# Attention's first steps in a four-layer adapter kernel: VectorE's order written out, token sums behind the divisors, a transfer split over two queues

## The chip, the cores and the metric

The kernel runs on one core of one Trainium2 chip. The metric is the device time of one execution in microseconds (us), as a median over runs. A profiled execution gives the trace that is read here; its engines are TensorE (PE; its weight loads are listed as PEld), VectorE (DVE), ScalarE (ACT), GpSimd (POOL) and SyncE (SP), which issues transfers.

## What is computed

Four residual layers over `x` of 8 sequences x 128 tokens x 512 features, all in float32: each is `x = x + ffn(cond(x))`. Layer 0 is a gated feed-forward network with low-rank adapters and a mixture of eight low-rank experts; layer 1 is an adapter and again eight experts; layer 2 is attention with a paged cache of keys and values, followed by a mixture; layer 3 is routed experts. The change lies at the end of layer 1 and in layer 2's attention:

```python
q = rope(rmsnorm(x @ Wq.T, q_norm_w), pos)          # 32 heads of 128
k = rope(rmsnorm(x @ Wk.T, k_norm_w), pos)          # 8 heads of 128
v = x @ Wv.T
kc, vc = k_cache[block_table], v_cache[block_table]  # 512 cached tokens, 8 heads
scores = q @ concat(kc, k).T / sqrt(128)             # cached tokens past the length masked
x = x + mixture(softmax(scores) @ concat(vc, v) @ Wo.T)
```

## The kernel before

**Steps.** Attention goes over 8 key heads (`qd`), and within one over 4 pairs of sequences (`p`): 32 steps `n`, each with two sequences `j` and four query heads. The projections of a step are a 2 x 2 block product done with seven products instead of eight (`seven`, lines 948 to 988): it needs sums of weight blocks (`factors`, line 871) and sums of token blocks (`tokens`, line 930, computed by `combine`, line 923). `seven` has named places (`one`, `u2`, `c22`, `c11`, `c12`) at which a caller can put other work into the program's order. After a projection come `squares` (ScalarE, sums of squares), `rotate` (products with the sine tables on GpSimd, line 1051; with the cosine tables on VectorE, line 1056), `roots` (ScalarE), `rotated` and `normed` (VectorE, lines 1068 to 1080) and `turn` (line 1103): VectorE transposes blocks of 32 x 32 of the queries and new keys into one tile, `written` (line 1096) sends that to DRAM in four transfers and `fetch` (line 1112) reads it back with the head dimension on the partitions. The cached keys go the same way in `turn_cached` (line 1087); both tiles share one buffer, the tag `kt` with `bufs=1`. `gather` (line 907) fetches cached keys and values by rows with GpSimd's transfers.

**A turn of the loop** (`run`, line 1254): `weigh` makes scores for one sequence, five key blocks each, and ScalarE takes their exponentials (lines 1124 and 1128); `added` sums the five blocks on VectorE (line 1144); `mix` multiplies with the values (line 1175); `summed` gets the divisors on TensorE (line 1153); `inverted` takes their reciprocals (line 1160), copies them into `R` (line 1163) and spreads them over the partitions with three transfers (line 1165). In the next step `divided` (line 1185) applies `R`, `outputs` computes the block sums `os` of the result, and `leave` is a second `seven` product with the output weights that adds into `y2`. Step `n`'s turn projects step `n+1`, and prepares the cached keys and token sums of step `n+2`.

**What sets the order.** Each engine runs its instructions in the order in which the build lists them. The build is free to reorder what is ready by its own reckoning, except that instructions passed to `keep_in_program_order` keep their order among themselves on their engine. `kept` (line 853) passes an instruction there if `running` is not empty, if its engine is GpSimd, or if `always` is given. `running` becomes true only in `run`, after steps 0 and 1 have been projected; so the first two steps' projections are ordered by the build, together with layer 1's expert products (`outs1`, TensorE and a sum into `x` on VectorE, line 300), which are never kept. Layer 1's experts end with `mix1(1)` (four transposes on TensorE and a copy) and `outs1(1)` (four products, whose banks have the tag `st` with three buffers; `seven`'s second product uses one of these too).

**First steps in the program's text before.** `att.first(0)` has step 0's token sums, projection, squares, rotation, the keys' gather for step 1, roots, turning and fetching; then `mix1(1)` and `outs1(1)`; then `run` calls `first(1)` for step 1. In the loop, step 0 computes `tokens(2)` and then `turn_cached(1)`, whose read of the cached keys is issued ahead of `fetch(1)`. Steps from 1 on compute `tokens(n + 2)` between `added` and `summed`, hence before `inverted`. There are token sums only where `qd` of step `n+2` is 0, 1 or 7: from 2 to 6 the sums of 1 are kept.

Of the kernel before, what the change touches and what calls it, by code (L numbers as in the profile page):

```python
# [17 lines left out]
P = 128  # L18
# [29 lines left out]
def forward(ctx: ExitStack, tc: tile.TileContext, a: dict, out: bass.AP):  # L48
# [615 lines left out]
    with psa:  # L664
# [46 lines left out]
        route1(1)  # L711
        att.first(0)
        mix1(1, small_bank)
        outs1(1, range(DC), large_bank)
        kept = nc.dram_tensor("kept_x", (P, DC, NT), F32, kind="Internal").ap()
# [70 lines left out]
def attention(tc, a, x, ident, lens, kvrow, part, ww, wop, ypool, sums, rot, eps, psa, c2, chunks, mm):  # L786
# [65 lines left out]

    def kept(i, always=False):
        return tc.keep_in_program_order(i) if always or running or i.ins.engine == pool.engine else i

# [37 lines left out]
    def every(ops):  # L893
        for _ in ops:
            pass
# [33 lines left out]

    def tokens(n):  # L930


        qd, p = steps[n]
        b = 2 * p
        if 0 < qd < NQ - 1 and p in kept_sums:
            S[n]["A"] = kept_sums[p]
            return
        parts = [x[:, 2 * h : 2 * h + 2, (b + j) * P : (b + j + 1) * P] for j in range(2) for h in range(2)]
        if 0 < qd < NQ - 1:
            if not kept_sums:  # L940
                late.append(late[0].tile([P, NP, 4, 2, P], F32, tag="yT", name="xs_all"))
            S[n]["A"], ops = combine(late[1][:, p], *parts)
            kept_sums[p] = S[n]["A"]
        else:
            S[n]["A"], ops = combine(wk.tile([P, 4, 2, P], F32, tag="xs", name=f"xs_{n}", bufs=1), *parts)
        every(ops)

# [133 lines left out]

    def turn_cached(n, always=False):

        s = S[n]
        t = wk.tile([P, 4, 8, 32], F32, tag="kt", name=f"kt_{n}", bufs=1)
        for j in range(2):
            kept(dve.transpose(
                t[:, :, 4 * j : 4 * j + 4, :], s["kc"][j].rearrange("p c (b d) -> p b c d", b=4)
            ), always)
        s["kT"] = wk.tile([P, 4, 8, 32], F32, tag="kT", name=f"kT_{n}")  # L1090
        written(turned[n], t)
        kept(sp.dma_start(s["kT"], turned[n].rearrange("b i a m d -> (b i) a m d")))

    def written(dst, t):
        for q in range(4):
            kept(sp.dma_start(dst[:, :, q].rearrange("b i m d -> i b m d"), t[32 * q : 32 * q + 32]))

    def turn(n):

        s = S[n]  # L1100
        m = 2 * REP
        t = wk.tile([P, 4, m + 2, 32], F32, tag="kt", name=f"qkt_{n}", bufs=1)
        kept(dve.transpose(t, s["both"].rearrange("p m (b d) -> p b m d", b=4)))
        s["qT"] = wk.tile([P, 4, m, 32], F32, tag="qT", name=f"qT_{n}", bufs=1)
        s["kn"] = wk.tile([P, 2, 4, 32], F32, tag="kTn", name=f"kTn_{n}", bufs=1)
        written(turned_new[n], t)

    def fetch(n):
        s = S[n]
        m = 2 * REP  # L1110
        src = turned_new[n].rearrange("b i a m d -> (b i) a m d")
        kept(sp.dma_start(s["qT"], src[:, :, 0:m, :]))
        for j in range(2):
            kept(sp.dma_start(s["kn"][:, j], src[:, :, m + j, :]))
# [122 lines left out]

    def first(n):
        tokens(n)
        project(n, {"u2": lambda: turn_cached(n, True)} if n == 0 else {})  # L1240
        for j in range(2):
            squares(n, "q", j, range(REP))
            squares(n, "k", j, range(1))
        rotate(n)()
        if n == 0:
            gather(1, "k")
        roots(n)
        rotated(n)
        normed(n)
        turn(n)  # L1250
        if n == 0:
            fetch(n)

    def run(pool_, end_of, bank, keep):
# [3 lines left out]
        pool.memset(y2, 0.0)  # L1258
        first(1)
        gather(1, "v")  # L1260
        running.append(True)
        end, prepared = None, iter(())
# [5 lines left out]
        for n, (qd, p) in enumerate(steps):  # L1268
# [3 lines left out]
            sums_of, outs = added(n, 0), iter(())  # L1272
            next(sums_of)
            if n:
                divided(n - 1)
                outs = outputs(n - 1)
                some(w_ops)()
            every(sums_of)
            if after:
                project(after, {  # L1280
                    "one": some(outs, 2),
                    "u2": lambda: (every(outs), every(w_ops), some(wo_ops)()),
                    "c22": lambda: (turn_cached(2) if n == 1 else None, some(wo_ops, 2)()),
                    "c11": lambda: (squares(after, "k", 0, (0,)), squares(after, "q", 0, (0, 1))),
# [19 lines left out]
            else:  # L1304
                tokens(2)
                turn_cached(1)
                gather(2, "k")
# [6 lines left out]
            if n == 0:  # L1314
                fetch(1)
            every(added(n, 1))
            if 0 < n < len(steps) - 2:
                if steps[n + 2][1] == 0:
                    w_ops = W[steps[n + 2][0]].factors()
                    some(w_ops, 2)()  # L1320
                tokens(n + 2)
            summed(n)
# [9 lines left out]
            if 0 < n < len(steps) - 2:  # L1332
                turn_cached(n + 2)
            if n == 3:
# [779 lines left out]
```

## Time and profile before

| | |
|---|---|
| runs before | 1568.65, 1560.52, 1567.32 us; median 1567.32 us |
| profiled execution | 1561.03 us, of which the span is 1559.2 us |
| mean granted TensorE clock | 0.995 |
| instructions | 18584 |
| VectorE, ScalarE, GpSimd busy | 1034.2, 538.1, 827.6 us |
| transfers | 169.89 MB, on average 109 GB/s |

How to read it: a line of the order of time has the start in the span, the duration, the engine, the line of the code, the operation, the tile written and the tiles read, the shapes and a count of like instructions; in brackets stands how long the engine had been idle before it, and what ended that idle time. A product in float32 is two instructions on TensorE. Project, attention and output products of a typical step take some 33 us. Steps 0 and 1 are projected between about 303 and 331 us, step 0's scores begin at 333.9 us, step 1's at 356.0 us, and the last step ends near 1400 us.

### The profile page before, as it was taken

What the parts mean: (1) busy time and instruction counts of PE and PEld (TensorE: products, weight loads), DVE (VectorE), ACT (ScalarE), POOL (GpSimd) and SP (SyncE); (2) the same over time, 40 slices, a digit from 0 to 9 for tenths busy, and PEclk for the clock granted to TensorE, in tenths of its full rate; (3) what the DMA queues carried; (4) which work ended last, traced back from release to release, by engine and by line L of the source; (5) the groups of instructions that cost most, each with busy time, mean ns of one, the idle gap of its engine ahead of it and who ended that gap; (6) DMA issues with size and microseconds to landing.
All of it is one profiled execution on the core that took longest, in us unless ns stands there. A gap on an engine that the chain in (4) does not pass through costs nothing.

```text
span 1559.2 us, 18584 instructions
## 1 busy us (share of the span) xinstructions
PE 1520.0 (97%) x5985; PEld 925.7 (59%) x5985; DVE 1034.2 (66%) x1963; ACT 538.1 (35%) x1324; POOL 827.6 (53%) x842
## 2 busy tenths in 40 slices
PE   9999999989999999999999999999999999999998
PEld 7888886445555555555555555555555555568643
DVE  4566334387787786777777687777777888743241
ACT  1111110143434544444543444543445443420210
POOL 1341105285765777776777766777767677610000
PEclk9999999999999999999999999999999999999999
DMA  9111002144546434553454454355444335421000
GB/s 302 42 42 31 1 0 65 43 118 123 162 118 189 137 108 121 153 174 103 127 159 124 124 145 145 101 149 163 129 137 141 103 101 149 144 65 62 0 21 36
DMA packets 156682, 169.89 MB, mean 109 GB/s; under 512 B 54144, under 2 KB 127040, under 8 KB 156448
## 3 DMA queue, kind: packets, MB, share of 16 engines
q1 hardware_dynamic: 138432, 131.60, 29.9%
q0 software_dynamic: 17056, 36.49, 7.9%
q8 instruction: 50, 0.82, 0.2%
q10 hardware_dynamic: 1088, 0.52, 0.1%
q14 instruction: 56, 0.46, 0.1%
HBM read 113.89 MB, written 42.07 MB: 100 GB/s over the span
## 4 chain that ended last, share of the span: by engine, by line
PE 85%; DVE 5%; DMA 4%; POOL 3%; issue 2%; ACT 1%; SPq 0%; ACTq 0%; DVEq 0%; POOLq 0%
PE st L1124 16%; PE av L1175 15%; PE g L362 8%; PE q_six L962 7%; PE wo_two L962 5%; PE q_one L962 5%; PE dn L362 5%; PE q_five L962 4%; PE wo_six L962 3%; PE wo_one L962 3%; PE eo_l L53 2%; PE z L53 2%; PE h L1679 2%; PE o L53 2%; PE midp_l L53 1%
## 5 line engine op out<-in xcount | busy, mean ns | idle before, releaser
L907 POOL DMA_INDIRECT kn<-in_k_cache,kvrow_k x256 | 282.9, 1105 | 73.3 <-issue 67.1
L1175 PE MATMUL av<-pT,vals 128*128 128x512 f32 x640 | 298.8, 597 | 0.0
L907 POOL DMA_INDIRECT vals<-in_v_cache,kvrow_v x256 | 258.1, 1008 | 73.4 <-issue 44.5
L1128 ACT ACTIVATE pT<-st,hide 128x512 f32<-128x512 f32 x256 | 175.9, 687 | 325.7 <-PE st L1124 325.7
L1124 PE MATMUL st<-qT,kT 128*128 128x512 f32 x512 | 237.7, 597 | 7.2 <-DMA qT<-turned_new 7.2
L1051 POOL TENSOR_TENSOR vq<-q,txq 128x256 f32<-128x256 f32 x128 | 118.7, 956 | 180.8 <-ACT sqq L1035 117.4
L1175 PEld LDWEIGHTS av<-pT,vals 128*128 128x128 f32 x640 | 119.0, 190 | 143.9 <-issue 141.5
L1124 PEld LDWEIGHTS st<-qT,kT 128*128 128x128 f32 x512 | 97.2, 191 | 117.4 <-issue 111.0
L1144 DVE TENSOR_TENSOR part<-pT 128x512 f32<-128x512 f32 x128 | 88.3, 692 | 82.7 <-ACT pT L1128 82.5
L962 PE MATMUL q_one<-q,x 128*128 128x384 f32 x256 | 93.0, 486 | 0.0
L1035 ACT ACTIVATE sqq<-q 128x128 f32<-128x128 f32 x256 | 79.3, 310 | 15.9 <-DVE q L1011 9.1
L1160 DVE RECIPROCAL rr<-sum 128x256 f32<-128x256 f32 x32 | 56.1, 1754 | 31.3 <-PE sum L1153 31.3
L962 PEld LDWEIGHTS q_one<-q,x 128*128 128x128 f32 x256 | 48.5, 190 | 39.8 <-issue 14.3
L962 PE MATMUL q_six<-q_s,xs_all 128*128 128x384 f32 x192 | 69.8, 486 | 0.0
L962 PE MATMUL wo_one<-o,oT 128*128 128x256 f32 x256 | 65.7, 379 | 0.0
L1124 PE MATMUL st<-qT,kTn 128*128 128x512 f32 x128 | 65.4, 592 | 0.0
L1016 ACT COPY q<-q_one 128x256 f32<-128x256 f32 x32 | 11.9, 372 | 153.4 <-PE q_one L962 144.5
L1213 POOL TENSOR_TENSOR y<-y,uo 128x512 f32<-128x512 f32 x32 | 41.3, 1291 | 43.3 <-DVE y L1205 42.8
L962 PE MATMUL wo_two<-o_s,os 128*128 128x256 f32 x256 | 60.5, 379 | 2.3 <-DVE os L923 2.3
L1128 ACT ACTIVATE pT<-st,rs 128x512 f32<-128x512 f32 x64 | 44.0, 687 | 38.4 <-PE st L1124 38.4
L962 PEld LDWEIGHTS wo_one<-o,oT 128*128 128x128 f32 x256 | 48.6, 190 | 13.4 <-PE st L1124 0.4
L1185 DVE TENSOR_TENSOR oT<-av,R 128x512 f32<-128x512 f32 x64 | 41.2, 685 | 21.6 <-DMA R<-R 21.3
(394 smaller groups left out, 2711.4 us busy)
## 6 DMA issues: line engine op xcount, KB each, us to landing
turned_new<-qkt SPq DMA_DIRECT2D x128, 160.0 KB
turned_cached<-kt SPq DMA_DIRECT2D x128, 128.0 KB
kT<-turned_cached SPq DMA_DIRECT2D x32, 512.0 KB
qT<-turned_new SPq DMA_DIRECT2D x32, 512.0 KB
R<-R SPq DMA_DIRECT2D x96, 128.0 KB
q<-in_WqT SPq DMA_DIRECT2D x8, 1024.0 KB
o<-in_WoT SPq DMA_DIRECT2D x8, 1024.0 KB
kn<-in_k_cache,kvrow_k POOLq DMA_INDIRECT x256, 3.0
```

The lines of the kernel that those rows point to most:

```text
L53: pe.matmul(o, lhsT, rhs, start=start, stop=stop)
L362: pe.matmul(o, lhsT, rhs, start=start, stop=stop, skip_group_check=True)
L907: kept(pool.indirect_dma_start(out=d[:, c, :], out_offset=None, in_=kc if what == "k" else vc, in_offset=bass.IndirectOffsetOnAxis(ap=kvro ...
L962: kept(pe.matmul(o, l[:, c, :], r[:, c, :], start=start and c == 0, stop=c == 1, skip_group_check=True))
L1035: kept(act.activation(sq, S[n][m][:, j, i, :], AF.Square, accum_out=S[n]["ssq"][:, j, col : col + 1]))
L1051: kept(pool.tensor_tensor(to, t[:, b, :, hi : hi + 64], wx[:, b, lo : lo + 64].unsqueeze(2).to_broadcast(list(to.shape)), ALU.mult,))
L1124: kept(pe.matmul(ps, s["kT"][:, c, 4 * j : 4 * j + 4, :] if c < 4 else s["kn"][:, j], s["qT"][:, :, REP * j : REP * (j + 1), :].rearrange( ...
L1128: kept(act.activation(pT[:, c, :, :].rearrange("p i t -> p (i t)"), ps, AF.Exp, **(dict(bias=hide[:, b, c : c + 1]) if c < 4 else dict(bia ...
L1144: kept(dve.tensor_tensor(o, l, r, ALU.add))
L1160: kept(dve.reciprocal(r, S[n]["sum"]))
L1175: kept(pe.matmul(ps, v[:, c, :], pT[:, c, :, :].rearrange("p i t -> p (i t)"), start=c == 0, stop=c == NC - 1, skip_group_check=True,))
L1213: kept(pool.tensor_tensor(t, t, u.unsqueeze(1).to_broadcast([P, 2, HW]), ALU.add))
```

## The change

- `first` now covers both first steps. `running` becomes true right after step 0's token sums, so everything in `first` that goes through `kept` holds the program's order.
- Step 1's token sums are computed at `c22` of step 0's projection, into a buffer with the tag `pT` instead of `xs`.
- Step 0's squares lie at `c11` and `c12` of its own projection. After it come `rotate(0)`'s first part, the keys' gather for step 1 and layer 1's `mix1(1)`. Step 1's projection follows, and behind its first product comes the rest of step 0: squares, roots, the keys' products, expert products 0 and 1 between the steps of the rotation, the turning, its four writes from SyncE's and ScalarE's queues in turn, and the fetch. Expert products 2 and 3 follow; their sums into `x` on VectorE are bound to come after the turning.
- `run` begins with three products into a bank that nobody reads (`idle_q`), then step 1's squares, rotation and turning.
- In step 0 of the loop `turn_cached(1)` comes ahead of `tokens(2)`, and the read of its result is issued after the read of step 1's queries instead of before it.
- In the loop, the token sums of step `n+2` move from before `summed` to behind `inverted` and `turn_cached(n + 2)`. A weight sum (`w_ops`) comes before `divided` instead of after it. The first two of the four `os` sums, which were at `one` of the projection, move to `u2` beside the other two.

The diff, without the lines that only follow from these (the argument `always` goes away):

```diff
@@ forward
         route1(1)
-        att.first(0)
-        mix1(1, small_bank)
-        outs1(1, range(DC), large_bank)
+        att.first(lambda: mix1(1, small_bank), lambda *o: outs1(1, o, large_bank))
@@ attention: turn_cached, written, turn, fetch
         written(turned[n], t)
-        kept(sp.dma_start(s["kT"], turned[n].rearrange("b i a m d -> (b i) a m d")))
+        return lambda: kept(sp.dma_start(s["kT"], turned[n].rearrange("b i a m d -> (b i) a m d")))
-    def written(dst, t):
+    def written(dst, t, by=(sp,)):
         for q in range(4):
-            kept(sp.dma_start(dst[:, :, q].rearrange("b i m d -> i b m d"), t[32 * q : 32 * q + 32]))
+            kept(by[q % len(by)].dma_start(dst[:, :, q].rearrange("b i m d -> i b m d"), t[32 * q : 32 * q + 32]))
-    def fetch(n):
+    def fetch(n, between=lambda: None):
         kept(sp.dma_start(s["qT"], src[:, :, 0:m, :]))
+        between()
         for j in range(2):
             kept(sp.dma_start(s["kn"][:, j], src[:, :, m + j, :]))
@@ first
-    def first(n):
-        tokens(n)
-        project(n, {"u2": lambda: turn_cached(n, True)} if n == 0 else {})
-        for j in range(2):
-            squares(n, "q", j, range(REP))
-            squares(n, "k", j, range(1))
-        rotate(n)()
-        if n == 0:
-            gather(1, "k")
-        roots(n)
-        rotated(n)
-        normed(n)
-        turn(n)
-        if n == 0:
-            fetch(n)
+    def first(mixed, outs_):
+        every(tokens(0))
+        running.append(True)
+        later = tokens(1, "pT")
+        project(0, {
+            "u2": lambda: turn_cached(0)(),
+            "c22": lambda: every(later),
+            "c11": lambda: (squares(0, "k", 0, (0,)), squares(0, "q", 0, (0, 1))),
+            "c12": lambda: squares(0, "q", 0, (2, 3)),
+        })
+        keys_terms = rotate(0)
+        gather(1, "k")
+        mixed()
+        def rest():
+            squares(0, "q", 1, range(REP))
+            squares(0, "k", 1, (0,))
+            roots(0)
+            keys_terms()
+            outs_(0)
+            rotated(0)
+            outs_(1)
+            normed(0)
+            turned_0 = turn(0, (sp, act))
+            fetch(0)
+            with tc.issue_after(turned_0.ins):
+                outs_(2, 3)
+        project(1, {"one": rest})
@@ run
-        first(1)
+        idle = psa.tile([P, 512], F32, tag="mm", name="idle_q", bufs=3)
+        for _ in range(3):
+            kept(pe.matmul(idle, x[:, 0, 0:P], x[:, 0, 0:512], start=True, stop=True))
+        for j in range(2):
+            squares(1, "q", j, range(REP))
+            squares(1, "k", j, (0,))
+        rotate(1)()
         gather(1, "v")
-        running.append(True)
+        roots(1)
+        rotated(1)
+        normed(1)
+        turn(1)
...
             next(sums_of)
+            some(w_ops)()
             if n:
                 divided(n - 1)
                 outs = outputs(n - 1)
-                some(w_ops)()
             every(sums_of)
             if after:
                 project(after, {
-                    "one": some(outs, 2),
                     "u2": lambda: (every(outs), every(w_ops), some(wo_ops)()),
...
             else:
-                tokens(2)
-                turn_cached(1)
+                read_cached = turn_cached(1)
+                every(tokens(2))
                 gather(2, "k")
...
             if n == 0:
-                fetch(1)
+                fetch(1, read_cached)
             every(added(n, 1))
-            if 0 < n < len(steps) - 2:
-                if steps[n + 2][1] == 0:
-                    w_ops = W[steps[n + 2][0]].factors()
-                    some(w_ops, 2)()
-                tokens(n + 2)
+            if 0 < n < len(steps) - 2 and steps[n + 2][1] == 0:
+                w_ops = W[steps[n + 2][0]].factors()
+                some(w_ops, 2)()
             summed(n)
             inverted(n)
...
             if 0 < n < len(steps) - 2:
-                turn_cached(n + 2)
+                turn_cached(n + 2)()
+                every(tokens(n + 2))
```

## The prediction

> **What bounds the kernel now.** I read the page's busy times and chain first, then TensorE's waits by releaser, then the order of time around each wait, then the granted clock. TensorE is the bound: the page gives it 97% of the span and 85% of the chain.
>
> ```profile
> PE 1520.0 (97%) x5985; PEld 925.7 (59%) x5985; DVE 1034.2 (66%) x1963; ACT 538.1 (35%) x1324; POOL 827.6 (53%) x842
> ...
> PE 85%; DVE 5%; DMA 4%; POOL 3%; issue 2%; ACT 1%; SPq 0%; ACTq 0%; DVEq 0%; POOLq 0%
> ```
>
> So only TensorE's idle time (1559.2 - 1520.0 = 39.2 us) and time at a lower clock can be won; VectorE's 66% is worth something only where a wait of TensorE ends on it. TensorE's waits (us in total, times, longest):
>
> ```profile
> PE st L1124 <- DMA qT<-turned_new: 7.2, 3, 3.5
> PE q_five L962 <- DVE uq L977: 3.5, 3, 1.2
> PE eo_l L53 <- DVE x L300: 2.4, 1, 2.4
> ...
> PE q_six L962 <- DVE vals L1011: 1.3, 3, 0.5
> ...
> PE q_six L962 <- DVE q_s L871: 0.6, 1, 0.6
> ```
>
> These are the ones that the diff can reach. In order of time, attention's first steps hold three:
>
> ```profile
> 320.48 1.37 PE L53 MATMUL eo_l<-midT_l,wB 128*128 128x512 f32 x2 [2.40 <-DVE x L300]
> ...
> 333.89 5.37 PE L1124 MATMUL st<-qT,kT 128*128 128x512 f32 x8 [3.50 <-DMA qT<-turned_new]
> ...
> 356.02 3.67 PE L1124 MATMUL st<-qT,kT 128*128 128x512 f32 x8 [2.26 <-DMA qT<-turned_new]
> ```
>
> The eight products at 333.89 take 5.37 us, those at 356.02 take 3.67: the clock fell. The busy time by stretch (length, then TensorE, weight load, VectorE, ScalarE, GpSimd, clock) shows two stretches at half clock, one after each of the first two waits:
>
> ```profile
> 321.25:324.60 3.35, 3.35 (x6) 1.70 (x6) 3.35 (x4) 0.00 (x0) 2.74 (x3) 0.50 0.17 54
> ...
> 334.90:338.25 3.35, 3.35 (x6) 1.27 (x5) 3.28 (x6) 1.37 (x2) 2.74 (x3) 0.50 0.17 44
> ```
>
> Each costs some 3.4 x 0.5 = 1.7 us. All that can be won here: 2.40 + 3.50 + 2.26 + 2 x 1.7 = 11.6 us. VectorE in the same time:
>
> ```profile
> 319.74 1.28 DVE L300 TENSOR_TENSOR x<-eo_l,x 128x512 f32<-128x512 f32 x2
> ...
> 323.34 1.50 DVE L1103 STREAM_TRANSPOSE qkt<-r 128x1280 f32<-128x1280 f32 x1
> ...
> 330.97 3.61 DVE L1056 TENSOR_TENSOR r<-q,tsq 128x1024 f32<-128x1024 f32 x1
> ...
> 343.79 1.30 DVE L1087 STREAM_TRANSPOSE kt<-kn 128x512 f32<-128x512 f32 x2
> ```
>
> The first sums into x (line 300) stand behind step 0's whole rotation, so the fourth expert product has no free bank. The turning of step 0's queries ends at 324.84 and TensorE gets them at 333.89, 9.05 us later.
>
> In the loop the other waits lie in three steps in which token sums are computed ahead of the divisors. In one:
>
> ```profile
> 1219.06 1.49 DVE L923 TENSOR_TENSOR xs<-x 128x256 f32<-128x256 f32 x1
> ...
> 1222.01 1.74 DVE L1160 RECIPROCAL rr<-sum 128x256 f32<-128x256 f32 x1
> ...
> 1230.06 1.29 DVE L1185 TENSOR_TENSOR oT<-av,R 128x512 f32<-128x512 f32 x2 [3.00 <-DMA R<-R]
> ```
>
> VectorE sits 3.00 us on R's transfer with all the next projection's sums behind it. TensorE loses 0.65 + 1.20 + 0.51 there, 1.20 + 0.51 at 434.76 and 436.82, 1.06 + 0.24 + 0.21 at 502.88 to 511.63: 5.6 us.
>
> **What the Trainium skill says.** "TensorE: Matmul & The Clock Gate", Part 1: the array falls to half clock after an idle window of about 3.4 us, and the windows run free of the program. The trace agrees in the length (0.50 over 3.35 us and more), but windows only partly idle (2.40 us) were enough here, and the 2.26 us before 356.02 brought no drop. "DMA: Bandwidth & Descriptors", Issuing engines are not separate DMA queues: transfers from several engines share the same DMA engines; only issue time is saved. The trace of before has one queue alone, 1.94 us for four writes. "SBUF — State Buffer", SBUF: two separate sides: VectorE with two inputs in SBUF and GpSimd lock each other out for whole instructions. That fits the 3.61 us product above, beside four GpSimd products; the same form took 1.31 at 370.20.
>
> **The change, part by part.**
>
> *Order in step 0.* Step 1's token sums move ahead of the projection's last sums, two sums into x instead of four stand before the turning, the other two behind. From the trace, the last sum of step 0's projection could end near 313.9 (TensorE ends that projection at 313.1). Then: 1.75 + 0.94 (products with the tables) + 0.69 (x) + 1.47 + 0.43 (rotation) + 0.69 (x) + 0.21 + 1.22 + 1.50 = 8.9, so the turning ends at 322.8, 2.0 earlier. If GpSimd locks it as above (3.61 for 1.75), 324.7, no gain.
>
> *Two queues.* Four issues in 1.94 us become two pairs side by side: at most 1.0 saved, at least 0, as the data share one set of DMA engines. I take 0.5. The two on ScalarE's queue wait for the turning; behind them stand the copies of step 1's queries, which come 8.9 us after ScalarE's last work in before, so that costs nothing; without that cover it would be two issues of 0.49. Scores of step 0 then start at 322.8 + 9.05 - 0.5 = 331.35 instead of 333.89: 2.5 won.
>
> *Expert products and step 1's projection.* The second product of step 1 now waits for the second sum into x, at 313.9 + 1.75 + 0.94 + 0.69 + 1.47 + 0.43 + 0.69 = 319.9; TensorE is through with the expert products at 318.1. An idle of 1.8 stays, but the path to the scores goes through the turning: the projection (6 x 1.29 = 7.7) ends at 327.6, ahead of them. A half clock here costs at most its 1.7 and is covered by that.
>
> *Idle products.* Three of two instructions, 0.43 apart: 2.6 us, 327.6 to 330.2, ahead of the scores in TensorE's queue. They hide under the wait up to 331.35 and leave 1.1 bare. What they buy is the half clock after 333.89: 1.7. Uncovered they would cost 2.6.
>
> *What is late next.* Step 1's rotation now starts near 328.7, not 330.97; its turning took until 339.32, 8.35 later, of which 1.9 is the lock: I take 336.2 (335.2 to 337.1). Its tile has one buffer, which the turning of step 1's cached keys shares and which is free when the four writes have landed, 4.5 later as in step 0 (324.84 to 329.36): 340.7. The change puts those keys ahead of the token sums, so VectorE would stand idle there; then keys 1.3, token sums 1.55, key-block sums 2.78: TensorE can sum the divisors at 346.5. It gets there 13.0 after the scores start (335.6 without the half clock, to 348.63): 344.4. A new wait of 2.1. From there to step 1's scores 5.1 (348.63 to 353.76): 351.6. The query read is now issued ahead of the cached keys' read, which lands by 350 to 352; so the 2.26 goes. 356.02 - 351.6 = 4.4 won in the first steps.
>
> *Token sums behind the divisors; weight sums ahead of the division; output sums after the projection's.* R leaves 3.1 to 4.0 earlier (what the four token sums took in each of those steps), and the token sums fill the wait for it. VectorE's work up to the projection's last sums is otherwise the same, so the delay falls by its idle time (2.1, 2.9, 3.0), more than the stalls that it causes. I leave 0.8 for what stays where weight sums stand before the division: 4.8 of 5.6. The output sums now lie between the projection's second sum and the one read by its last product. In steps with a weight sum there too, that product's inputs are ready 7.6 after the projection's start; it is due at 7.7. So 0, with 0.5 a step if this is misjudged.
>
> *Sum.* 4.4 + 4.8 = 9.2. The profiled execution took 1561.03 (span 1559.2 and 1.8 around it): 1551.8. The median shown, 1567.32, is 6.3 higher; the executions lie in two places (1560.52 and 1561.03; 1567.32 and 1568.65), and nothing says where the next median falls. I take the middle of 1561.03 and 1567.32, 1564.2: **1555**. About 0.5% (7.8 us) is what a measurement can tell from no change.
>
> **Rivals.** *The wait moves to VectorE (1560):* GpSimd's lock holds step 0's and 1's rotation, and the new wait at the divisors' sum eats what the scores won. For it: 3.61 us, the single buffer. Against: the order gives slack of 2 us. Some 1 + 3 = 4 won. *All goes (1550):* the sums into x, which no order binds, are put into VectorE's gaps; keys come in time: 11.6 - 2.6 + 5.2 = 14. Against it: the single buffer. *Slower (1570):* output sums ahead of the sum that the projection's last product reads. Spare is 0.1 to 1.7 us; if TensorE waits 0.5 in each of 30 steps, 15 lost against 9.2 won, 1564.2 + 5.8. It decides from 0.31 a step. Against: VectorE's work there is the same in both orders. *It does nothing:* the order written down is the one built before; the trace excludes it (sums at 319.74).
>
> **Numbers.** Forecast (gain 6 to 13): 0.50, of which 0.41 is over 7.8; wait moves: 0.30; all goes: 0.12; slower: 0.08. Faster 0.41 + 0.12 = 0.53; slower 0.08; same 0.39. Range: from 1546 (14 off 1560.5) to 1566 (2 off 1568), which leaves out the slower case and some of the ends.
>
> **What would show it.** Turning of step 0 ends near 322.8; scores start near 331.4 with no half clock after; a wait of sum on part in step 0 near 344; no 2.26 wait in step 1; no q_five or q_six waits near 434, 502 and 1232. Wrong: q_six waiting on vals in many steps, idle products running on past the queries' landing, or that turning later than 324.

## The result and the profile after

The median of 15 runs went from 1565.06 us (1560.52 to 1569.85) to 1560.36 us (1556.56 to 1562.78): a ratio of 0.9967, with an interval of 0.9954 to 0.998. That is 4.7 us, half of the 9.2 that were forecast. The profiled execution took 1556.86 us, its span is 1555.1 us.

The page first: TensorE's busy time, in which the six idle instructions and the time at half clock count, is lower by 0.5 us only. Most of the difference between the two traces is idle time (1555.1 - 1519.5 = 35.6 us instead of 39.2).

```profile
PE 1519.5 (98%) x5991; PEld 928.9 (60%) x5991; DVE 1025.3 (66%) x1963; ACT 538.0 (35%) x1324; POOL 829.0 (53%) x842
...
PE 87%; DVE 5%; DMA 3%; POOL 2%; issue 1%; ACT 1%; SPq 0%; ACTq 0%; DVEq 0%; POOLq 0%
```

TensorE's waits by releaser (us in total, times, longest), after:

```profile
PE sum L1155 <- DVE part L1146: 4.7, 2, 3.5
PE wo_six L962 <- DVE y L1207: 4.0, 10, 0.8
PE st L1126 <- DMA qT<-turned_new: 2.8, 2, 1.6
...
PE q_six L962 <- DVE x L300: 1.1, 1, 1.1
...
PE q_six L962 <- DVE vals L1011: 0.3, 1, 0.3
```

The wait on the turned queries fell from 7.2 to 2.8, and the one of the fifth products on `uq` (3.5) is gone. New are a wait of 3.5 at the divisors' sum, on VectorE's key-block sums, and short ones of the output products on `y` (4.0 in ten places; 2.2 in five before).

Four marks in TensorE's order split the span: A, the first product of step 0's projection; the scores of step 0; those of step 1; and the last turned output products (`y2T`) after the loop.

| stretch, us | before | after | after, another chip |
|---|---|---|---|
| start to A | 303.72 | 301.05 | 304.05 |
| A to step 0's scores | 30.17 | 27.89 | 27.86 |
| step 0's scores to step 1's | 22.13 | 23.31 | 22.74 |
| step 1's scores to `y2T` | 1054.58 | 1049.35 | 1050.09 |
| `y2T` to the end | 148.64 | 153.47 | 153.50 |

So in these traces the first steps gave 1.1 us (1.7 on the other chip), not 4.4; the loop gave 5.2 (4.5, with 1.7 lost to a half clock in it), where 4.8 was said; and the end, which the prediction did not touch, took 4.8 back. Each column is a single execution; the section on the end compares its 4.8 with all runs. What lies ahead of A is the same work in all fourteen traces of this study and came out between 300.1 and 305.3 us. The 2.7 there is no effect of the change: the kernel before had two stretches of 3.4 us at half clock there, the changed one none.

The first steps in TensorE's order of time, after:

```profile
324.61 2.74 PE L1279 MATMUL idle_q<-x 128*128 128x512 f32 x6
328.94 3.67 PE L1126 MATMUL st<-qT,kT 128*128 128x512 f32 x8 [1.60 <-DMA qT<-turned_new]
...
341.98 0.43 PE L1155 MATMUL sum<-part,ones 128*32 128x128 f32 x8
345.89 0.65 PE L1155 MATMUL sum<-part,ones 128*32 128x128 f32 x8 [3.48 <-DVE part L1146]
...
352.25 3.60 PE L1126 MATMUL st<-qT,kT 128*128 128x512 f32 x8
```

The eight first scores take 3.67 us, not 5.37: no half clock there. But the second half of the divisors' sum waits 3.48, and half clock follows that wait. In the busy times by stretch (length, then TensorE, weight load, VectorE, ScalarE, GpSimd, clock) it is the first line, and a second such stretch lies near the end, where the kernel before had none:

```profile
345.90:349.25 3.35, 3.35 (x12) 1.42 (x13) 2.57 (x4) 0.00 (x0) 2.48 (x3) 0.50 0.94 258
1441.60:1451.80 10.20, 10.20 (x41) 10.20 (x41) 0.00 (x0) 0.58 (x2) 0.00 (x0) 0.50 0.01 2
```

VectorE ahead of the new wait:

```profile
330.20 1.47 DVE L1068 TENSOR_TENSOR r<-r,vq 128x1024 f32<-128x1024 f32 x1 [3.31 <-POOL vq L1051]
...
340.37 1.30 DVE L1087 STREAM_TRANSPOSE kt<-kn 128x512 f32<-128x512 f32 x2 [2.30 <-DMA turned_new<-qkt]
```

It stands idle twice: 3.31 us for GpSimd's sine products in step 1's rotation, then 2.30 us for the shared `kt` buffer. GpSimd in the same time:

```profile
315.73 1.17 POOL L905 DMA_INDIRECT kn<-in_k_cache,kvrow_k  x1 [0.15 <-issue]
...
325.38 2.00 POOL L905 DMA_INDIRECT kn<-in_k_cache,kvrow_k  x1 [0.30 <-issue]
327.40 2.77 POOL L1051 TENSOR_TENSOR vq<-q,txq 128x256 f32<-128x256 f32 x4
```

The eight gathers of step 1's keys fill its queue from 315.73 to 327.38. Step 1's queries are complete at 325.23, the sine products begin at 327.40. In the kernel before, the gathers began at 319.52, and the last of them and the sine products were:

```profile
328.95 0.94 POOL L907 DMA_INDIRECT kn<-in_k_cache,kvrow_k  x1 [0.30 <-issue]
329.91 2.76 POOL L1051 TENSOR_TENSOR vq<-q,txq 128x256 f32<-128x256 f32 x4
```

The sine products began 26.2 us after A there and begin 26.4 after A now. This point of GpSimd's queue did not move, although step 1's queries are complete 24.2 us after A now and were at 27.1 before.

In the loop, VectorE's order in the step that the prediction showed:

```profile
1215.01 1.31 DVE L1165 COPY R<-rr 32x256 f32<-32x256 f32 x4
...
1218.67 0.42 DVE L921 TENSOR_TENSOR xs<-x,xs 128x256 f32<-128x256 f32 x1
...
1221.59 1.28 DVE L1187 TENSOR_TENSOR oT<-av,R 128x512 f32<-128x512 f32 x2
```

The token sums lie inside R's transfer, and the division waits for nothing (3.00 before). From its scores to those of the next, the three steps with the waits that the prediction listed (3, 5 and 27) took 35.27, 36.75 and 36.17 us before and take 33.01, 34.98 and 33.01 now: 7.2 won. The other steps of the loop together lost 2.0.

### The profile page after: what moved, and what is told of

Its sections match the earlier page's. It is cut to its first block, busy times and chain, and to the rows that moved or that the text cites. A ratio compares the mean times of both kernels' runs of the same rounds, so it can differ in the third digit from the quotient of the medians.

```text
span 1555.1 us, 18566 instructions
## 1 busy us (share of the span) xinstructions
PE 1519.5 (98%) x5991; PEld 928.9 (60%) x5991; DVE 1025.3 (66%) x1963; ACT 538.0 (35%) x1324; POOL 829.0 (53%) x842
## 4 chain that ended last, share of the span: by engine, by line
PE 87%; DVE 5%; DMA 3%; POOL 2%; issue 1%; ACT 1%; SPq 0%; ACTq 0%; DVEq 0%; POOLq 0%
PE av L1177 17%; PE st L1126 16%; PE q_six L962 7%; PE g L362 7%; PE q_one L962 5%; PE q_five L962 5%; PE wo_two L962 5%; PE dn L362 5%; PE wo_six L962 3%; PE wo_one L962 3%; PE eo_l L53 2%; PE z L53 2%; PE h L1704 2%; PE o L53 2%; PE midp_l L53 1%
## 5 line engine op out<-in xcount | busy, mean ns | idle before, releaser
L1177 PE MATMUL av<-pT,vals 128*128 128x512 f32 x640 | 300.1, 600 | 0.0
L1130 ACT ACTIVATE pT<-st,hide 128x512 f32<-128x512 f32 x256 | 175.9, 687 | 328.7 <-PE st L1126 328.7
L362 PE MATMUL g<-xs,ws 128*128 128x256 f32 (+1 forms) x240 | 55.2, 379 | 1.4 <-POOL ws L429 1.4
```

Of the source, the lines that this page charges most:

```text
L362: pe.matmul(o, lhsT, rhs, start=start, stop=stop, skip_group_check=True)
L1130: kept(act.activation(pT[:, c, :, :].rearrange("p i t -> p (i t)"), ps, AF.Exp, **(dict(bias=hide[:, b, c : c + 1]) if c < 4 else dict(bia ...
L1177: kept(pe.matmul(ps, v[:, c, :], pT[:, c, :, :].rearrange("p i t -> p (i t)"), start=c == 0, stop=c == NC - 1, skip_group_check=True,))
```

## The experiments

Twelve kernels ran, in three groups of four, each group on one chip beside runs of the kernel before. Traces exist of the twelve, not of the kernel before on these chips. The stretches of every trace, in us:

| kernel | group | A to scores 0 | scores 0 to scores 1 | to `y2T` | to the end |
|---|---|---|---|---|---|
| first steps alone | 1 | 27.92 | 23.58 | 1066.43 | 155.31 |
| loop alone | 1 | 30.19 | 22.18 | 1072.78 | 147.84 |
| key gather split | 1 | 27.71 | 20.28 | 1075.69 | 155.27 |
| own buffer | 1 | 27.97 | 20.93 | 1072.64 | 153.63 |
| changed kernel | 2 | 27.86 | 22.74 | 1050.09 | 153.50 |
| output sums back | 2 | 28.01 | 23.50 | 1049.16 | 155.37 |
| three edits | 2 | 27.59 | 20.28 | 1048.08 | 155.96 |
| one queue | 2 | 28.22 | 21.56 | 1052.11 | 153.73 |
| no idle products | 3 | 27.91 | 23.17 | 1048.80 | 154.48 |
| before, with idle products | 3 | 30.75 | 21.97 | 1057.28 | 157.33 |
| best | 3 | 27.75 | 19.71 | 1046.33 | 151.37 |
| token sums in the gap | 3 | 28.30 | 22.60 | 1049.84 | 155.20 |

### First steps alone, loop alone

The changed kernel with the loop's edits taken back, and the kernel before with only those:

```diff
 first steps alone, against after
-            some(w_ops)()
             if n:
                 divided(n - 1)
                 outs = outputs(n - 1)
+                some(w_ops)()
...
+                    "one": some(outs, 2),
...
+                every(tokens(n + 2))
             summed(n)
...
-                every(tokens(n + 2))
```

> The change's first steps, with the loop's order as before (token sums ahead of the divisors, weight sum after the division, two output sums ahead of the projection's sums). Read by two distances in the trace: D1 from step 0's first projection product to step 1's first scores (52.3 us before, 51.2 after), D2 from there to the first transposing product on y2 (1054.6 before, 1049.4 after). If the loop's gain and the first steps' gain are separate: D1 as after, 51.2, D2 as before, 1054.6, and the time 1 us or less under before. If the loss sits in the loop (rival), D2 would be longer than before's 1054.6.

> The loop's new order alone, first steps as before. If the two are separate: D1 52.3, D2 about 1049.4 and the time some 5 us under before, as much as the whole change. Rival, that the loop's gain depends on the first steps' order: D2 stays near 1054.

Measured: 1578.66 us (1575.91 to 1584.22) and 1578.23 (1568.61 to 1584.78), beside 1577.25 of the kernel before on that chip: ratios 1.0004 (0.9989 to 1.002) and 1.0003 (0.9979 to 1.0027). Neither half gains there. The second distance, from step 1's scores to `y2T`, cannot be read as the expectations meant it: 1066 us with the old order of the loop and 1073 with the new one (3.4 of it lost at half clock in each) are both longer than the 1054.6 that the old order took in the first trace. The first steps alone take 51.50 us from A to step 1's scores, with a wait of 3.71 at the divisors' sum; the loop alone, with the old first steps, 52.37. In the traces the loop's new order is 6 us slower than the old one on this chip, where it was 5 us faster in the first traces. The times show less: by its interval the loop alone is at most some 4 us slower than the kernel before. VectorE and TensorE beside one such wait, loop alone:

```profile
672.16 0.56 DVE L977 TENSOR_TENSOR uq<-q_five,uq 128x384 f32<-128x384 f32 x1 [2.52 <-PE q_one L962]
```

```profile
667.92 1.45 PE L962 MATMUL q_five<-q_s,xs_all 128*128 128x384 f32 x4
...
672.78 1.56 PE L962 MATMUL q_five<-q,xs_all 128*128 128x384 f32 x4 [0.82 <-DVE uq L977]
```

The fifth product ends at 669.37; the sum that reads it begins at 672.16, although VectorE had been idle for 2.52 us. Where VectorE had been idle ahead of this sum, the median of the distance is 1.10 us here, 1.57 in the trace of the first steps alone, and 0.04 in the kernel before and in the changed kernel's first trace. So VectorE is late at the output sums, which now stand ahead of the sums for the last product, and the sixth products wait 8.3 us on `vals` (0.3 in the changed kernel's first trace). The durations of nearly all instructions are the same on both chips. This is the mechanism of the rival "slower", on one chip.

The steps keep the edits apart. In steps 3, 5 and 27 the loop alone takes 104.1 us and the old order 108.6: the token sums win 4.5 on this chip too. Steps 6 to 25 compute no token sums; only the output sums, and in some steps a weight sum, stand elsewhere in them. They take 675.2 us in the loop alone and 666.3 in the old order: 8.9 lost. On the other chips these steps take 662.0 to 662.6 us with the output sums in the old place (five traces) and 662.9 to 663.9 in the new one (five).

### What holds step 1's turning: gather and buffer

Key gather split (second half behind step 1's sine products), and step 1's turned keys in a buffer of another tag:

```diff
 key gather split
-        gather(1, "k")
+        gather(1, "k", (0,))
         mixed()
...
         rotate(1)()
+        gather(1, "k", (1,))
         gather(1, "v")
 own buffer
-        t = wk.tile([P, 4, 8, 32], F32, tag="kt", name=f"kt_{n}", bufs=1)
+        t = wk.tile([P, 4, 8, 32], F32, tag="R" if n == 1 else "kt", name=f"kt_{n}", bufs=1)
```

> The change, with the second sequence's half of the gather of step 1's cached keys put behind step 1's rotation on GpSimd. Theory: the wait of 3.5 us at the divisors' sum in step 0 comes from GpSimd's queue: step 1's sine products stand behind eight key transfers. Then VectorE's turning of step 1 ends about 3.5 us earlier against the scores, the wait falls to under 0.3 us, no half clock follows, and D1 falls from 51.2 to 46 or 47. Rival (the shared buffer and the token sums alone make the wait): the turning of step 1 moves but the wait stays over 2 us, D1 49 or more.

> The change, with step 1's cached keys turned in another buffer than step 1's queries. VectorE's idle time of 2.3 us ahead of that turning goes. Theory (the wait is made of GpSimd's queue, buffer and token sums one after another): the wait at the divisors' sum falls from 3.5 to about 1.2 us, and with no half clock after it D1 falls from 51.2 to 47 to 49. If the buffer were the whole cause, the wait would go to 0.

Measured, on the chip of the two above: the wait at step 0's divisors' sum fell from 3.71 to 1.34 and to 1.06, and step 1's scores came 47.99 and 48.90 us after A, 3.5 and 2.6 earlier than with the first steps alone. With the split, VectorE's idle time on the sine products is 0.61 instead of 3.31. The split's result lies between its two theories (under 0.3, over 2); the own buffer's is the one expected. Neither is the whole cause. The wait falls by 2.4 and by 2.7, together more than all of it, so the two overlap. The times (1580.96 and 1581.61, one run each) say nothing of it: on this chip TensorE then waited 3.8 and 2.0 us for step 1's exponentials, which started late too.

### The changed kernel again, output sums back, three edits, one queue

```diff
 output sums back, against after
                 project(after, {
+                    "one": some(outs, 2),
                     "u2": lambda: (every(outs), every(w_ops), some(wo_ops)()),
 three edits: the above, the split gather, and
-                read_cached = turn_cached(1)
                 every(tokens(2))
+                read_cached = turn_cached(1)
 one queue
-            turned_0 = turn(0, (sp, act))
+            turned_0 = turn(0)
```

> The changed kernel once more, to see whether the loop's gain is a property of the order or of one chip. In the first trace of it the reciprocal began 0.07 us after the last key-block product of the divisors' sum, in every step but three; in the four later traces, which came from one other chip, 0.3 to 1.1 us after it. Theory 1 (the loop's order is worth what the slack of VectorE at the output sums allows, and that slack is eaten where the reciprocal starts late): if the reciprocal starts late again, the waits of the projection's sixth products on vals and of the output products on uq come to over 8 us in the loop, and the loop from step 1's scores to the end's first turning takes over 1070 us, with a ratio of 0.998 to 1.002; if it starts at 0.07 us, those waits stay under 1 us, the loop takes about 1049 us and the ratio is near 0.9967. Theory 2 (the order gains whatever the start of the reciprocal): ratio near 0.997 in both cases.

Measured: 1561.48 us (1558.45 to 1565.26) beside 1565.72, ratio 0.9983 (0.9971 to 0.9996). On this chip the reciprocal begins 0.06 to 0.15 us after the products again, the loop takes 1050 us (1.7 of it a half clock at 1369.8) and no projection waits on `vals` for over 0.3 us. Theory 1 holds for the waits and the loop; the gain in time is real, and a little smaller than the 0.9967 that it said.

> The changed kernel with the first two groups of output sums put back behind the projection's first product; the token sums stay behind the divisors. Theory 1 (all output sums at the projection's second product put VectorE late for the sixth product): the waits of the sixth products on vals and of the fifth on uq, and the 0.28 us waits of wo_six on y, fall to under half of those of the changed kernel in the same call; time lower by 1 to 5 us where the reciprocal starts late, the same within 1 us where it does not. Theory 2 (the token sums' new place is what makes VectorE late): the waits stay as they are, and the time too.

Measured: 1558.38 us (1553.18 to 1561.55), ratio 0.9959 (0.9946 to 0.9971). The waits of `wo_six` on `y` fell from 3.7 to 2.2 us, not to under half. Steps 3, 5 and 27 take 33.01, 34.81 and 33.01 us here too: the token sums made the loop's gain. The move of the output sums only cost: 3.1 us by the medians, where theory 1 said the same within 1 us on such a chip. The traces place 0.9 of it in the loop. The first steps of this one trace were 0.9 slower, so from A to `y2T` the two are equal (1100.67 and 1100.69); where the rest lies is open.

> Three edits of the changed kernel together: step 1's key gather split so that only half of it stands ahead of step 1's sine products on GpSimd; step 2's token sums ahead of step 1's cached keys, so that VectorE has work while the shared buffer is read; two groups of output sums back behind the projection's first product. Theory 1 (GpSimd's queue and the shared buffer made the new wait at the divisors' sum): no wait over 0.5 us at the divisors' sum of step 0, step 1's scores 46.5 to 48.0 us after step 0's first product of the projection (51.2 in the changed kernel, 52.3 in the one before), the time 3 to 6 us below the changed kernel in the same call. Theory 2 (the exponentials of step 1 are late for another reason, as in the run with the split gather alone, and take it back): the first steps gain 3 us or more, and ScalarE's pT costs them again within 10 us; the time within 1.5 us of the changed kernel.

Measured: 1557.13 us (1553.04 to 1560.84), ratio 0.9945 (0.9928 to 0.9962), 4.4 below the changed kernel. Step 1's scores come 47.87 after A, not 50.60, and the wait at step 0's divisors' sum is 0.21 instead of 2.82. Most of the gain in time, 3.1, came with the output sums already; the other two edits add 1.2 by the medians. Theory 1 holds for the wait and the scores, with one thing that it had not: TensorE now waits 1.7 us on the read of step 1's cached keys, which is behind the shared buffer as before.

> The changed kernel with the four writes of step 0's turned queries on one queue again. Theory 1 (the read waits for the data of the last write, not for its issue, so a second queue buys nothing): step 0's scores start 27.9 us after the projection's first product, within 0.2, as with two queues. Theory 2 (issue was on the path, as the prediction took it): 28.4 or later.

Measured (one run, 1562.69 us): scores 28.22 after A: 0.36 later than with two queues in the trace above. SyncE's queue in this kernel:

```profile
323.82 1.94 SPq L1096 DMA_DIRECT2D turned_new<-qkt  x4
328.83 0.65 SPq L1113 DMA_DIRECT2D qT<-turned_new  x1
```

and in the changed one, SyncE's and then ScalarE's:

```profile
319.59 0.78 SPq L1096 DMA_DIRECT2D turned_new<-qkt  x2
324.19 0.65 SPq L1113 DMA_DIRECT2D qT<-turned_new  x1
```

```profile
319.60 0.85 ACTq L1096 DMA_DIRECT2D turned_new<-qkt  x2
```

The issue takes 0.86 instead of 1.94. The read is issued 4.60 to 4.66 after the turning in the ten traces with two queues, and 4.52, 4.52, 4.93 and 5.04 after it in the four with one. Step 0's scores come 27.59 to 28.30 after A in those ten, so 28.22 decides for neither theory: the second queue is worth at most 0.4, within what one queue differs from trace to trace. Step 1's scores are even earlier here, 49.78 after A. The Trainium skill, "DMA: Bandwidth & Descriptors", Issuing engines are not separate DMA queues, has it that only the time of issue is saved; here even of those 1.1 us little arrived.

### The end: no idle products, and only idle products

From `y2T` to the end the traces so far lie at 153.5 to 156.0 us with the idle products and at 147.8 and 148.6 without. The suspicion: `idle_q` takes one place in the rotation of the banks tagged `mm`, and everything later in that rotation lands one bank further.

```diff
 no idle products, against after; before with idle products has the same lines behind first(1)
-        idle = psa.tile([P, 512], F32, tag="mm", name="idle_q", bufs=3)
-        for _ in range(3):
-            kept(pe.matmul(idle, x[:, 0, 0:P], x[:, 0, 0:512], start=True, stop=True))
```

> The changed kernel without the idle products and their PSUM tile. Theory 1 (the tile moves the rotation of the three banks that it shares by one, so that 1100 us later the first product of the end's turned weights, W3p, meets a bank that four sums into x free and not two, waits 1.97 us instead of 0.77, and the window after it is taken to half clock): W3p waits 0.77 us, no half clock near 1440 us, from the last turned output products to the end 148 to 149 us instead of 153.5, and the time 4 to 5 us below the changed kernel. A half clock of 1.7 us after the first scores may return; it falls in front of the wait at the divisors' sum and step 1's scores come at the same distance within 1 us. Theory 2 (the half clock near the end comes from the order of the first steps, whatever the banks): the end stays at 153 to 155 us, the time within 1 us of the changed kernel or up to 2 us above.

> The kernel before with the six idle instructions alone, in the tile and at the place where the changed kernel has them (behind step 1's projection, ahead of the first scores). Theory 1 (bank rotation): W3p waits 1.97 us, the end takes 153 to 155 us instead of 148.6, the time 3 to 5 us above the kernel before, less up to 1.7 us if the half clock after the first scores goes. Theory 2: the end stays at 148.6 us, the time equal or 1.7 us lower.

Measured: 1558.08 us (1553.05 to 1560.01), ratio 0.9958 (0.994 to 0.9976), without them; 1571.92 (1566.64 to 1575.22), ratio 1.0044 (1.0024 to 1.0063), for the kernel before with them alone. The turned weights' products near the end, in this order: before, after, before with idle products, after without:

```profile
1442.95 1.85 PE L1892 MATMUL W3p<-ident,base 128*128 128x128 f32 x12 [0.77 <-DVE x L1857]
```

```profile
1435.15 1.53 PE L1917 MATMUL W3p<-ident,base 128*128 128x128 f32 x12 [1.97 <-DVE x L1882]
```

```profile
1446.33 1.81 PE L1895 MATMUL W3p<-ident,base 128*128 128x128 f32 x12 [1.97 <-DVE x L1860]
```

```profile
1434.19 1.85 PE L1914 MATMUL W3p<-ident,base 128*128 128x128 f32 x12 [0.77 <-DVE x L1879]
```

Adding the products with their tile makes 1.97 of 0.77, and leaving them out makes 0.77 of 1.97: the 1.2 us are shown, in all ten traces with them and all four without. The first bank is free after four of VectorE's sums into `x` with the tile (2.5 us) and after two without (1.3), as the rotation would have it; products and tile were not tried apart. The half clock behind it is not settled as expected. With 1.97, all ten traces have 10.2 to 17.1 us of half clock there; with 0.77, two have none and two have 6.8 and 13.7, although TensorE's waits there (0.77, 0.74, 0.46) are the same in one with none and in the one with 13.7. So the longer wait makes it surer, and is not its only cause. The trace without idle products still took 154.48 from `y2T` to the end: theory 1 missed there. And the kernel before lost more by them than either theory said: 8.1 us by the medians, 157.33 at the end.

The traces' 4.8 at the end can be set against all runs, since each run's mean granted clock is on record. One minus it, times the span, estimates the time lost at low clock (not all of it delays the end, since some is followed by a wait). A run's clock is rounded to 0.001, 1.6 us, so only means count:

| kernel | group, runs | mean clock | lost at low clock, us | mean time less that, us |
|---|---|---|---|---|
| before | 1, 27 | 0.9913 | 13.8 | 1564.0 |
| first steps alone | 1, 14 | 0.9905 | 15.0 | 1564.0 |
| loop alone | 1, 14 | 0.9926 | 11.7 | 1566.3 |
| before | 2, 52 | 0.9925 | 11.7 | 1553.5 |
| changed kernel | 2, 22 | 0.9920 | 12.5 | 1549.2 |
| output sums back | 2, 22 | 0.9923 | 12.0 | 1546.2 |
| three edits | 2, 15 | 0.9923 | 12.0 | 1544.9 |
| before | 3, 16 | 0.9934 | 10.4 | 1553.5 |
| no idle products | 3, 8 | 0.9930 | 10.9 | 1546.7 |
| before, with idle products | 3, 7 | 0.9907 | 14.6 | 1556.8 |
| best | 3, 6 | 0.9943 | 8.8 | 1542.5 |

By the two traces with which the study began, the changed kernel should lose 3.4 us more at low clock behind A than the kernel before: 5.1 more at the end, 1.7 less in the first steps. On the second chip it loses 0.8 more (plus or minus 1.2). So about half of the 4.8, or more, belongs to the executions that were traced and not to the change; the trace of the kernel before has a high clock for that kernel (0.995) and no half clock near 1440 us. Apart from the clock the change wins 4.3 us, with the output sums back 7.3, and without the idle products 6.9. By this estimate the output sums' move costs 3.0 (plus or minus 0.7) and the idle products cost 2.6 (plus or minus 1.1, from two chips). In the kernel before, the idle products cost 3.2 and another 4.2 at low clock.

What the idle products bought is seen in the traces with and without them. Half clock behind step 0's scores: in 3 of 10 traces with them, in 4 of 4 without. But without them the wait at the divisors' sum is 1.78 instead of 3.48, less by the 1.7 of the half clock. No half clock follows it; the scores wait 1.33 for the cached keys' read in its place, and come 51.08 after A, as with the idle products (51.20).

### The rest: best, and token sums in the gap

Best is the split gather, the own buffer and the output sums back, without idle products. The last kernel is the changed one with step 2's token sums ahead of step 1's cached keys (shown above).

> The changed kernel with the key gather split, step 1's turned keys in a buffer of their own, two groups of output sums back behind the projection's first product, and no idle products. Theory 1: no wait over 0.7 us at the divisors' sum, step 1's scores 46.0 to 48.0 us after the projection's first product, the end 148 to 149 us; the time 8 to 10 us below the changed kernel, ratio to the kernel before 0.990 to 0.992. Theory 2 (the end's half clock is not the tile's): 4 to 5 us below the changed kernel, ratio 0.994 to 0.995.

Measured: 1552.01 us (1544.92 to 1556.22), ratio 0.9918 (0.9895 to 0.9941): 11.8 below the kernel before, and 6.1 below the changed kernel without idle products. That is theory 1, except that the end took 151.37 with 6.8 of half clock in it. VectorE and TensorE in it:

```profile
329.34 1.46 DVE L1067 TENSOR_TENSOR r<-r,vq 128x1024 f32<-128x1024 f32 x1 [0.61 <-POOL vq L1050]
...
338.34 1.30 DVE L1086 STREAM_TRANSPOSE kt<-kn 128x512 f32<-128x512 f32 x2
```

```profile
344.83 0.64 PE L1154 MATMUL sum<-part,ones 128*32 128x128 f32 x16
```

The sixteen products of the divisors' sum run as one group, with no wait; step 1's scores come 47.46 after A.

> The changed kernel with step 2's token sums ahead of step 1's cached keys, and nothing else. Theory 1 (VectorE stands idle for the shared buffer, 2.3 us in the trace of the changed kernel, and the 1.6 us of token sums fit in there): the wait at step 0's divisors' sum falls from 2.8 to 3.6 us to 1.2 to 2.2 us and step 1's scores come 1.3 to 1.6 us earlier, less where the half clock falls behind the wait. Theory 2 (the wait comes from GpSimd's queue alone): unchanged.

Measured: 1562.60 us (one run). The wait at the divisors' sum is gone: the key-block sums are done 15.0 after step 0's scores instead of 16.9, and a half clock behind those scores took 1.7 of what TensorE had waited. But now the scores of step 1 wait, and half clock follows:

```profile
355.76 4.94 PE L1126 MATMUL st<-qT,kT 128*128 128x512 f32 x7 [2.59 <-DMA kT<-turned_cached]
```

They come 50.90 after A: 0.3 won against the first trace of the changed kernel and none against the second (50.60), not 1.3 to 1.6. The cached keys are turned 39.3 after A in both kernels, when the shared buffer comes free, and their read lands some 50.9 after A. So the wait at the sum had covered a second one of nearly the same length, behind the same buffer. Theory 1 was right on the first and blind to the second.

## Why the prediction was right and wrong, step by step

- **Order in step 0: right.** The turning ended 18.5 after A (19.1 predicted). VectorE's product with the cosine table took 1.25, not the 1.75 of the sum or the 3.61 of the lock. Beside it GpSimd's four sine products took 3.96, where four with VectorE idle took 2.77: if this is the lock, it held GpSimd here. (The product of 1.31 at 370.20, which the prediction set against 3.61, ran beside two sine products too, and these took 2.40.) Two of the four sums into `x` stand in front of the turning, as planned, and 1.07 of the 1.8 stayed at the second projection product.
- **Two queues: mis-sized.** 0.5 was taken; the issue of the read gained between 0.4 and -0.1, and the read then took longer: 9.38 from the turning to the scores, where 8.55 was said and 9.05 had been measured. So the scores come 0.26 later than said, although the turning ended 0.6 earlier.
- **Idle products: the mechanism right, the worth wrong.** They were hidden and mostly kept the clock. But the half clock that they avoid lies ahead of a wait for VectorE, and what TensorE gains in front of that wait, it waits longer there (3.48 against 1.78). The prediction priced 1.7 for it and then found that wait itself, two steps on. It saw their time and not their tile, which costs 1.2 us at the end and, in the kernel before, brought half clock there.
- **"What is late next": the step that failed.** It put step 1's turning at 336.2 - 328.7 = 7.5 after the start of its rotation, with VectorE's lock as the only other party. It was 10.0 (325.35 to 335.37): the lock was absent (1.22 for the product), but the sine products stood behind eight gathers in GpSimd's queue, and VectorE waited 3.31. The prediction had the gather in front of it and never read that queue. The shared buffer was seen and came free 5.0 after the turning (4.5 said). So the key-block sums were done 16.9 after step 0's scores, where 15.15 was said: a wait of 3.48, not 2.1. A half clock behind it, which made the way to step 1's scores 1.26 longer, was not counted. 0.26 (scores) + 1.75 + 1.26 = 3.3: that is what is missing between 47.9 from A to step 1's scores, as predicted, and 51.2. Behind it stood a second wait: the cached keys' read, for which the prediction had 350 to 352, lands 50.9 after A in the last experiment, 354.6 in the prediction's time. The split gather brings back 3.5 by itself, the own buffer 2.6.
- **Loop: right in cause, and in size partly by luck.** 4.8 was said, 5.2 and 4.5 measured; the division finds R there. But the three steps with the listed waits won 7.2, more than their 5.6 of waits, and the other steps lost 2.0. The term that was put at 0, the output sums' new place, is not 0: it costs about 1 us in steps 6 to 25 of the traces, and 3 by the runs. The margin of 0.1 us at the last product (7.6 against 7.7) was real: on the chip where TensorE's signals come late it is overrun, and in the traces these steps lose 8.9 us.
- **Sum.** 9.2 was said and 4.7 measured. In the traces 6.3 were won from A to `y2T`, 3.3 less than said in the first steps, and the end gave 4.8 back, of which the runs bear out half at most. Two costs that the prediction did not count show in the runs: the output sums' move (3.0) and the idle products (2.6). These are estimates, from different chips, and do not sum exactly.
- **Rivals.** "The wait moves to VectorE" has the size that came (4 won), and named the divisors' sum; but the lock, its cause, did not hold VectorE there. "Slower" shows its mechanism in the loop on one chip, at 6 us in the traces instead of 15.

Open: why signals came late on one chip, and what the whole change is worth there, which was not run; what decides on half clock near the end when the waits are the same; where all of the 3.1 us of the output sums' return lie.

## What to carry to other kernels

When a chain is started earlier, read every in-order queue that it passes, GpSimd's gathers too, up to the point where it meets the next shared buffer. Before adding filler products, ask whether a wait for another engine follows that absorbs the lost time anyway, as it did here, and look at the waits of the far end, since their tile takes a place in a rotation of banks. An order with a margin of a tenth of a microsecond should be tried on more than one chip. And a difference between two traces is one of two executions: set it against the clocks of all runs before it is called an effect of the change.

## What the runs showed of the hardware that was not expected

- Between chips, the time from TensorE's end to VectorE's start differs while the durations of nearly all instructions do not: where the reciprocal had to wait for the divisors' products, it began 0.06 to 0.3 us after them in all traces but those of group 1, and mostly 0.3 to 1.1 us after them there. The kernel before took 1577.25 us on that chip, and 1563.77 to 1565.72 in the other comparisons.
- Half clock moves from run to run. "TensorE: Matmul & The Clock Gate", Part 1, in the Trainium skill says that the windows run free of the program; the traces agree: ahead of A, where the work is the same, it fell at 27.7 and 249.5 us in the kernel before, at 93.2 in the changed one on another chip, and nowhere in its first trace.
